# Values projected in five chunks of 128 keys and one split over column tiles, with new constants for the order of the work

## The chip, the core and the metric

The kernel runs on one core of a Trainium2 chip. A core has a matrix engine (PE, whose weight loads are listed apart as PEld), a vector engine (DVE), a scalar engine (ACT), a general engine (POOL) and a queue that only issues transfers (SP). Each works through its own list of instructions in order; semaphores hold an instruction until what it needs is there. The metric is the device time of one execution in microseconds (us); lower is better. The kernel before takes 619.33 us, the median of three runs (619.13, 619.33 and 622.4).

## The reference

One layer of cross-attention and one FFN over 8 batches of 100 queries and 722 context rows (keys), 512 features, 16 heads of 32. The attention weights come from sparsemax, not softmax: each row of scores is cut at a bound tau so that what lies above it sums to one.

```
def sparsemax(x):
    x = x - jnp.max(x, axis=-1, keepdims=True)
    zs = -jnp.sort(-x, axis=-1)
    L = x.shape[-1]
    rho = jnp.arange(1, L + 1, dtype=x.dtype)
    cssv = jnp.cumsum(zs, axis=-1) - 1.0
    support = zs > cssv / rho
    k = jnp.maximum(jnp.sum(support, axis=-1, keepdims=True), 1)
    tau = jnp.take_along_axis(cssv, k - 1, axis=-1) / k.astype(x.dtype)
    return jnp.clip(x - tau, 0.0)
...
vh = _split_heads(v @ Wv + bv)
scores = jnp.einsum('bhqd,bhkd->bhqk', qh, kh) * scale
attn = sparsemax(scores)
out = jnp.einsum('bhqk,bhkd->bhqd', attn, vh)
return out @ Wo + bo
...
real = jnp.einsum('bti,io->bto', x, jnp.cos(theta + theta_noise))
imag = jnp.einsum('bti,io->bto', x, jnp.sin(phi + phi_noise))
return jnp.sqrt(real * real + imag * imag)
...
x = x + xattn(layernorm(x), ctx_1024, ctx_1024, ...)
x = x + ffn(layernorm(x), ...)
```

## The kernel before

**Steps of a batch.** Tokens are normalised in tiles of 128 rows that run over batch borders (`TILES`), transposed and multiplied into queries. The context comes in transposed, features on the partitions. The steps of one batch, with the engine that does each:

- keys (PE, line 559): for each of four groups of features and two halves of the keys, four matmuls of 361 columns, with a bias copy on ACT (line 570). In batch 0 the first six of these run as the context arrives (line 548).
- scores, called fill (PE, lines 606 and 617): 32 by 32 tiles of the array, sixteen at a time, into one large PSUM tile `psc`. Five fills a batch. ACT copies each into `s_t` (line 628, two buffers).
- tops (DVE, line 639): 8 largest of every segment of 30 or 31 scores, 312 instructions a batch, then rests, candidates and a first bound (lines 648 to 697).
- five rounds to the bound of sparsemax: compare on DVE (`above`, line 706), product on POOL (line 711), count and sum on DVE (lines 717 and 727), small updates (lines 728 to 732).
- parts: POOL splits the bounds into three bfloat16 parts (lines 747 to 764), PE transposes them (line 769), ACT copies them out (lines 778 to 793).
- values (PE, line 581): the keys are cut into 6 chunks, five of 121 and one of 117 (`CK`, `NC`). A chunk is four accumulating matmuls, the chunk's context columns as the stationary operand, 512 feature columns moving. ACT copies the chunk to `v_t` (line 594).
- weights (PE, lines 813 and 826): minus the bound, then keys times queries on four row tiles, five pairs of feature group and key chunk a time (`PAIRS`), with the keys on the partitions. ACT takes the relu (line 838).
- outputs (PE, line 849): weights times values on four column tiles of 32 features each; ACT adds the bias (line 863).
- once a token tile is complete: output product, residual, second norm, two FFN products (line 502), squares on ACT, sum on POOL, root on ACT, result on POOL and its transfer out.

The weights of the FFN are made on POOL and ACT in the first batches (lines 419 to 437). After the loop the program tests whether the bounds were safe, and has a slower second path for the case that they weren't.

**Order.** A planner (`Plan`) writes out one order for all engines before anything is issued. A step is a `Task` with an engine and a cost from the table `STEPS`; edges say what it waits for, and `hold` says which buffers it takes and who frees them (four PSUM banks `pm`, one `psc`, and so on). A greedy loop takes, engine by engine, the step that can start first, and among those the one due first. The due time is the batch number times `PERIOD`, less the length of the longest chain behind the step, plus a constant for its kind from `LAG`; `STAY` is what a PE step gains in that comparison when it has the same tiling as the one before it (`SHAPE`). So the constants change only the order in which each engine meets its instructions, and, with the order, who waits for whom. The values of a batch are needed only by its outputs, so the planner is free to lay them between other PE work. Weights need the relu of the batch before in ACT and the one `psc`, so between weights and their outputs PE is given another product.

Of the kernel before, what the change touches and what calls it, by code (L numbers as in the profile page):

```python
# [11 lines left out]
FP = mybir.dt.float32  # L12
# [8 lines left out]
B, Q, S, DM = 8, 100, 722, 512  # L21
HD = 32
P = 128
NG = DM // P
# [19 lines left out]
def fills_of(left_first):  # L44
# [112 lines left out]
LAG = {  # L157
    "above": 260.0,
    "above count": -180.0,
    "above values": -150.0,  # L160
    "add bo": -5.0,
    "bounded": -75.0,
    "candidates": -190.0,
    "checks": 30.0,
    "deviation": 165.0,
    "ffn": 300.0,
    "fill": -240.0,
    "fill copy": 30.0,
    "fill last": -235.0,
    "first bound": 270.0,  # L170
    "keys": -65.0,
    "keys bias": 280.0,
    "keys part": -285.0,
    "leftovers": 250.0,
    "load bias": 205.0,
    "load ctx": 295.0,
    "load part": 120.0,
    "load w": 200.0,
    "load x": -160.0,
    "load x again": 180.0,  # L180
    "losses": 250.0,
    "normed": -80.0,
    "normed 2": -110.0,
    "normed T": -65.0,
    "normed copy": -245.0,
    "output product": 235.0,
    "outputs": -205.0,
    "outputs bias": 70.0,
    "parts": -180.0,
    "parts T": -165.0,  # L190
    "parts copy": -240.0,
    "parts copy last": -285.0,
    "queries": -285.0,
    "queries bias": -215.0,
    "residual": -55.0,
    "rests": 130.0,
    "result": 150.0,
    "sines": -300.0,
    "square": -215.0,
    "square sum": 275.0,  # L200
    "stats": 100.0,
    "stats 2": 265.0,
    "tops": 240.0,
    "turned": 160.0,
    "turns": -255.0,
    "update": 55.0,
    "update far": 155.0,
    "values": 110.0,
    "values copy": -200.0,
    "weights": -80.0,  # L210
    "weights relu": 300.0,
}


# [108 lines left out]
def xattn_ffn(  # L323
# [18 lines left out]
    nc = tc.nc  # L342
# [7 lines left out]
    ps1 = ctx.enter_context(tc.tile_pool(name="ps1", bufs=4, space=PSUM))  # L350
# [224 lines left out]
        )  # L575

    def values(st, c):
        n = min(CK, S - c * CK)
        st["pv", c] = pv = ps1.tile([P, DM], FP, name="pm")
        for k in range(NG):  # L580
            nc.tensor.matmul(  # L581
                pv[:n],
                lhsT=st["c"][:, k, c * CK : c * CK + n],
                rhs=wv_sb[:, k, :],
                start=(k == 0),
                stop=(k == NG - 1),
            )

    def values_copy(st, c):

        if "v" not in st:
            st["v"] = big.tile([P, NC, DM], FP, name="v_t")
        n = min(CK, S - c * CK)
        nc.scalar.copy(st["v"][:n, c, :], st.pop(("pv", c))[:n])  # L594

# [369 lines left out]
    for b in range(B):  # L965
# [239 lines left out]
    with tc.If(flag > 0):  # L1205
        with tc.For_i(0, B) as b:
# [20 lines left out]
            for c in range(NC):  # L1227
                values(st, c)
                values_copy(st, c)
            st["top"] = top = small.tile([P, NT], FP, name="top")  # L1230
            st["t", 0] = t_all = small.tile([P, NT], FP, name="t_all", bufs=1)
            st["th"] = small.tile([P, NC3 + 1, HG], FP, name="th")
# [96 lines left out]
```

## Time and profile before

| | |
|---|---|
| median of three runs | 619.33 us |
| profiled execution, its own time | 617.21 us |
| its span | 615.6 us |
| PE busy | 590.9 us (96%), 6497 matmul records |
| DVE busy | 520.5 us (85%) |
| ACT busy | 257.5 us (42%) |
| POOL busy | 226.3 us (37%) |
| granted PE clock over the span | 0.994 |
| values, matmuls (line 581) | 384 records, mean 600 ns |
| values, copies (line 594) | 48, mean 586 ns |
| outputs (line 849) | 1536 records, mean 251 ns |

The span is the stretch that the profiler covers. Busy is the time in which at least one instruction of an engine ran; matmuls overlap, so the mean of a record is longer than its share of the busy time, and the distance from one group's first record to the next group's is a better price. Each fp32 matmul leaves two records. The chain of waits, followed back from the last instruction, runs 46% through PE and 39% through DVE, in turns.

### The profile page before, as it was taken

The page shows a single profiled execution, that of the slowest core. Times are in us where ns is not written, and L with a number is a line of the kernel's source. Part 1 is how long each engine was busy: PE and PEld are TensorE (multiplying, and loading weights), DVE is VectorE, ACT ScalarE, POOL GpSimd, SP SyncE. Part 2 cuts the span into 40 slices and gives each one's busy share as a digit, 9 for nine tenths or more (in the row PEclk, how much of TensorE's full clock was granted, in tenths as well). Part 3 has the DMA queues.
Part 4 walks back from the last instruction along what each step waited for, and adds up shares of the span by engine and source line. Part 5 has one row for each costly group of instructions (what it writes and reads, how often), then busy time and mean ns, then how long its engine had stood idle before and what let it go on. Part 6 is the DMA issues. An engine that isn't in the chain of part 4 may idle for free.

```text
span 615.6 us, 17162 instructions
## 1 busy us (share of the span) xinstructions
PE 590.9 (96%) x6497; PEld 330.5 (54%) x6497; DVE 520.5 (85%) x3198; ACT 257.5 (42%) x355; POOL 226.3 (37%) x296
## 2 busy tenths in 40 slices
PE   5999999899999999999999999999999999999974
PEld 3755445556555655566466644675457434555531
DVE  2079999999999999997899989998999899998210
ACT  1244542355354435441644343552545334443521
POOL 1688487765500450024311650025211440165021
PEclk9999999999999999999999999999999999999998
DMA  8920012002000110002010102000030000000000
GB/s 307 364 92 19 18 56 78 18 19 98 19 2 3 40 60 2 3 2 97 19 37 2 41 2 98 3 2 1 3 132 3 0 23 2 2 20 2 2 18 21
DMA packets 12264, 26.56 MB, mean 43 GB/s; under 512 B 1856, under 2 KB 1856, under 8 KB 12176
## 3 DMA queue, kind: packets, MB, share of 16 engines
q1 hardware_dynamic: 11664, 23.77, 11.3%
q0 software_dynamic: 512, 1.64, 0.7%
q8 instruction: 53, 0.87, 0.6%
q14 instruction: 35, 0.29, 0.2%
HBM read 23.76 MB, written 1.64 MB: 41 GB/s over the span
## 4 chain that ended last, share of the span: by engine, by line
PE 46%; DVE 39%; issue 7%; POOL 5%; ACT 1%; DMA 1%; SPq 0%; POOLq 0%; DVEq 0%; ACTq 0%
DVE cand L639 19%; PE pm L581 12%; PE pm L559 12%; PE pm L502 5%; DVE f L727 4%; DVE m L706 4%; PE psc L826 3%; PE pm L849 3%; PE psc L617 3%; DVE n L717 3%; PE pm L479 3%; POOL p L711 3%; PE psc L548 2%; DVE rest L648 1%; DVE t L674 1%
## 5 line engine op out<-in xcount | busy, mean ns | idle before, releaser
L639 DVE MAX8 cand<-s_t 128x8 f32<-128x30 f32 x2496 | 230.3, 174 | 3.5 <-ACT s_t L628 3.5
L711 POOL TENSOR_TENSOR p<-z,m 128x1040 f32<-128x1040 f32 (+2 forms) x50 | 89.1, 1785 | 271.4 <-DVE m L706 269.7
L581 PE MATMUL pm<-wv_sb,c_t 128*121 128x512 f32 (+1 forms) x384 | 174.7, 600 | 0.0
L559 PE MATMUL pm<-c_t,wk_sb 128*128 128x361 f32 x464 | 150.9, 473 | 0.0
L559 PEld LDWEIGHTS pm<-c_t,wk_sb 128*128 128x128 f32 x464 | 84.5, 189 | 52.3 <-issue 7.6
L581 PEld LDWEIGHTS pm<-wv_sb,c_t 128*121 128x121 f32 (+1 forms) x384 | 67.2, 183 | 82.8 <-issue 78.3
L838 ACT ACTIVATE aT<-psc 121x2000 f32<-121x2000 f32 (+1 forms) x40 | 70.8, 1771 | 53.6 <-PE psc L826 53.6
L628 ACT COPY s_t<-psc 128x1924 f32<-128x1924 f32 (+2 forms) x40 | 69.0, 1725 | 47.9 <-DVE cand L639 23.7
L594 ACT COPY v_t<-pm 121x512 f32<-121x512 f32 (+1 forms) x48 | 28.1, 586 | 93.8 <-PE pm L581 93.8
L570 ACT ACTIVATE k_t<-pm,bk_sb 128x361 f32<-128x361 f32 x60 | 33.6, 565 | 71.1 <-PE pm L559 70.9
L727 DVE TENSOR_REDUCE f<-p 128x13 f32<-128x1040 f32 (+2 forms) x50 | 50.7, 1013 | 9.5 <-POOL p L711 9.5
L717 DVE TENSOR_REDUCE n<-m 128x13 f32<-128x1040 bf16 (+2 forms) x50 | 50.7, 1013 | 1.1
L826 PE MATMUL psc<-q_t,k_t 32*121 32x100 f32 (+1 forms) x1536 | 46.8, 262 | 0.0
L849 PEld LDWEIGHTS pm<-aT,v_t 121*32 121x32 f32 (+1 forms) x1536 | 32.7, 109 | 24.7 <-issue 21.7
L826 PEld LDWEIGHTS psc<-q_t,k_t 32*121 32x121 f32 (+1 forms) x1536 | 45.9, 180 | 0.2
L617 PE MATMUL psc<-k_t,q_t 32*32 32x481 f32 (+1 forms) x1536 | 43.2, 474 | 0.0
L849 PE MATMUL pm<-aT,v_t 121*32 121x100 f32 (+1 forms) x1536 | 41.7, 251 | 1.2 <-ACT aT L838 1.2
L479 PEld LDWEIGHTS pm<-hT,wq_sb 128*128 128x128 f32 x224 | 28.2, 191 | 8.2 <-issue 6.3
L479 PE MATMUL pm<-hT,wq_sb 128*128 128x128 f32 (+1 forms) x224 | 29.5, 277 | 0.0
L502 PE MATMUL pm<-cos_sb,hT 128*128 128x512 f32 (+1 forms) x56 | 27.5, 636 | 0.7 <-ACT hT L469 0.7
L518 POOL TENSOR_TENSOR sq<-sq 128x512 f32<-128x512 f32 (+1 forms) x7 | 8.8, 1264 | 48.7 <-ACT sq L515 48.6
L617 PEld LDWEIGHTS psc<-k_t,q_t 32*32 32x32 f32 x1536 | 13.9, 103 | 23.1 <-issue 15.4
(298 smaller groups left out, 570.9 us busy)
## 6 DMA issues: line engine op xcount, KB each, us to landing
c_t<-in_ctx SPq DMA_DIRECT2D x7, 1444.0 KB, 6.3
x_t<-in_x SPq DMA_DIRECT2D x12, 256.0 KB, 2.9
out<-sq POOLq DMA_DIRECT2D x6, 256.0 KB, 2.9
c_t<-in_ctx SPq DMA_DIRECT2D x4, 361.0 KB, 6.2
wk_sb<-in_L_xattn_Wk SPq DMA_DIRECT2D x4, 256.0 KB, 5.5
wq_sb<-in_L_xattn_Wq SPq DMA_DIRECT2D x4, 256.0 KB, 6.3
cos_sb<-in_L_ffn_theta SPq DMA_DIRECT2D x4, 256.0 KB, 3.9
n_t<-in_L_ffn_theta_noise SPq DMA_DIRECT2D x4, 256.0 KB, 3.6
```

The source lines that it names most:

```text
L479: nc.tensor.matmul(tk["pq"][:, g, : tk["n"]], lhsT=wq_sb[:, c, g * P : (g + 1) * P], rhs=tk["hT"][:, c, :], start=(c == 0), stop=(c == NG ...
L559: nc.tensor.matmul(pk, lhsT=wk_sb[:, c, g * P : (g + 1) * P], rhs=st["c"][:, c, i * SH : (i + 1) * SH], start=(c == 0), stop=(c == NG - 1),)
L581: nc.tensor.matmul(pv[:n], lhsT=st["c"][:, k, c * CK : c * CK + n], rhs=wv_sb[:, k, :], start=(k == 0), stop=(k == NG - 1),)
L617: nc.tensor.matmul(psc[b * HD : (b + 1) * HD, j, at : at + EDGE[hi] - EDGE[lo]], lhsT=st["q"][r, g, qb * HD : (qb + 1) * HD], rhs=st["k"][ ...
L628: nc.scalar.copy(s_t[:, :, :n], st["psc"][:, :, :n])
L639: nc.vector.max(st["cand"][:, n, k, :], st["s", f][:, j, at + EDGE[k] - first : at + EDGE[k + 1] - first],)
L711: nc.gpsimd.tensor_tensor(st["p"][:, lo:hi], st["z"][:, lo:hi], st["m"][:, lo:hi], ALU.mult)
L717: nc.vector.tensor_reduce(n_t, st["m"][:, lo:hi], AX.X, ALU.add)
L727: nc.vector.tensor_reduce(s_t, st["p"][:, lo:hi], AX.X, ALU.add)
L826: nc.tensor.matmul(psc[:m, j, k * Q : (k + 1) * Q], lhsT=st["k"][r, g, lo : lo + m], rhs=st["q"][r, g, :], start=False, stop=(k == len(PAI ...
L838: nc.scalar.activation(st["aT", n][:CK, :, :w], st["psw"][:CK, :, :w], AF.Relu, scale=SCALE)
L849: nc.tensor.matmul(st["po", g][j * HD : (j + 1) * HD, :Q], lhsT=st["v"][:m, c, f : f + HD], rhs=aT[:m, j, k * Q : (k + 1) * Q], start=(c = ...
```

## The change

The values are cut into five chunks of 128 keys and a last one of 82. The 82 are computed as 64 keys and then 18 keys. For the 64, the array is used as two column tiles of 64: both have the same 64 keys, and each computes half of the 512 features, so its result has 64 partitions and 256 columns in PSUM, the two halves one below the other. For the 18, four column tiles of 32 each compute a quarter of the features (128 columns). Copying it out now takes six ACT copies, which also move the halves and quarters back side by side. The last chunk becomes a kind of its own for the planner (`values last`), its copy waits for the first chunk's copy, and the cost of a fill over two groups is set higher. `STAY`, `PERIOD` and nearly all of `LAG` have new values. Weights, relu and outputs follow `CK` and `NC`: chunks of 128 keys and one of 82 (`S - 5 * 128`).

```
-CK = 121
+CK = P
 NC = 6
+CL = S - (NC - 1) * CK
+CA = 64
+CB = CL - CA
...
+    "values last": ("PE", 2.7),
+    "values last copy": ("ACT", 2.0),
...
-SHAPE = {"fill": 1, "fill last": 2, "outputs": 2, "weights": 3}
+SHAPE = {"fill": 1, "fill last": 2, "outputs": 2, "values last": 2, "weights": 3}
-STAY = 175.0
-PERIOD = 121.0
+STAY = 50.0
+PERIOD = 96.0
...
-    "values": 110.0,
-    "values copy": -200.0,
-    "weights": -80.0,
-    "weights relu": 300.0,
+    "values": 220.0,
+    "values copy": 20.0,
+    "values last": 195.0,
+    "values last copy": 100.0,
+    "weights": -40.0,
+    "weights relu": -95.0,
...
     def values(st, c):
-        n = min(CK, S - c * CK)
         st["pv", c] = pv = ps1.tile([P, DM], FP, name="pm")
         for k in range(NG):
             nc.tensor.matmul(
-                pv[:n],
-                lhsT=st["c"][:, k, c * CK : c * CK + n],
+                pv,
+                lhsT=st["c"][:, k, c * CK : (c + 1) * CK],
                 rhs=wv_sb[:, k, :],
...
+    def values_last(st):
+        st["pv", NC - 1] = pv = ps1.tile([P, DM], FP, name="pm")
+        lo = (NC - 1) * CK
+        for m, n, at in ((CA, CA, 0), (CB, HD, DM * CA // P)):
+            w = DM * n // P
+            for k in range(NG):
+                for j in range(P // n):
+                    nc.tensor.matmul(
+                        pv[j * n : j * n + m, at : at + w],
+                        lhsT=st["c"][:, k, lo : lo + m],
+                        rhs=wv_sb[:, k, j * w : (j + 1) * w],
+                        start=(k == 0),
+                        stop=(k == NG - 1),
+                    )
+            lo += m
...
+    def values_last_copy(st):
+        pv = st.pop(("pv", NC - 1))
+        for lo, m, n, at in ((0, CA, CA, 0), (CA, CB, HD, DM * CA // P)):
+            w = DM * n // P
+            for j in range(P // n):
+                nc.scalar.copy(
+                    st["v"][lo : lo + m, NC - 1, j * w : (j + 1) * w],
+                    pv[j * n : j * n + m, at : at + w],
+                )
...
-                    tiles=FS,
+                    tiles=FS * (1.0 if len(cs) == 1 else 1.4),
...
-            v = add("values", lambda st=st, c=c: values(st, c), *c_in, *w["v"])
-            e = add("values copy", lambda st=st, c=c: values_copy(st, c), v)
+            if c < NC - 1:
+                v = add("values", lambda st=st, c=c: values(st, c), *c_in, *w["v"])
+                e = add("values copy", lambda st=st, c=c: values_copy(st, c), v)
+            else:
+                v = add("values last", lambda st=st: values_last(st), *c_in, *w["v"])
+                e = add("values last copy", lambda st=st: values_last_copy(st), v, vs[0])
```

More of the change, by code (lines that the diff above doesn't have):

```diff
@@ L149 @@
 }
-SHAPE = {"fill": 1, "fill last": 2, "outputs": 2, "weights": 3}
+SHAPE = {"fill": 1, "fill last": 2, "outputs": 2, "values last": 2, "weights": 3}
 CHANGE = (0.19, 0.1, 0.1, 0.1)
-STAY = 175.0
-PERIOD = 121.0
+STAY = 50.0
+PERIOD = 96.0
 WINDOW = 0.0
 LAG = {
[L158 to L178, printed above, removed]
-    "load x": -160.0,
[L180 to L207, printed above, removed]
-    "values": 110.0,
-    "values copy": -200.0,
-    "weights": -80.0,
-    "weights relu": 300.0,
@@ new lines @@
+    "above count": 105.0,
+    "above values": -195.0,
+    "add bo": 55.0,
+    "bounded": 300.0,
+    "candidates": 230.0,
+    "checks": 235.0,
+    "deviation": 40.0,
+    "ffn": 200.0,
+    "fill": -115.0,
+    "fill copy": -275.0,
+    "fill last": -110.0,
+    "first bound": -85.0,
+    "keys": -70.0,
+    "keys bias": -120.0,
+    "keys part": -100.0,
+    "leftovers": -270.0,
+    "load bias": -60.0,
+    "load ctx": 215.0,
+    "load part": -100.0,
+    "load w": -105.0,
+    "load x": -160.0,
@@ new lines @@
+    "load x again": 110.0,
+    "losses": 285.0,
+    "normed": 300.0,
+    "normed 2": -190.0,
+    "normed T": -165.0,
+    "normed copy": -195.0,
+    "output product": 285.0,
+    "outputs": -115.0,
+    "outputs bias": 115.0,
+    "parts": -115.0,
+    "parts T": -125.0,
+    "parts copy": 240.0,
+    "parts copy last": -265.0,
+    "queries": -295.0,
+    "queries bias": -130.0,
+    "residual": -60.0,
+    "rests": 5.0,
+    "result": -225.0,
+    "root": -20.0,
+    "sines": 285.0,
+    "square": 185.0,
@@ L212 @@
+    "square sum": 20.0,
+    "stats": 20.0,
+    "stats 2": 125.0,
+    "tops": 230.0,
+    "turned": -10.0,
+    "turns": 250.0,
+    "update": 120.0,
+    "update far": 85.0,
+    "values": 220.0,
[4 more added lines that the diff above has]
+    "weights relu": -95.0,
 }
@@ L592, in values_copy @@
             st["v"] = big.tile([P, NC, DM], FP, name="v_t")
-        n = min(CK, S - c * CK)
-        nc.scalar.copy(st["v"][:n, c, :], st.pop(("pv", c))[:n])
+        nc.scalar.copy(st["v"][:, c, :], st.pop(("pv", c)))
+    def values_last_copy(st):
[7 more added lines that the diff above has]
+                )
     def fill(st, f):
@@ L1226, in xattn_ffn @@
                     keys_bias(st, g, i)
-            for c in range(NC):
+            for c in range(NC - 1):
                 values(st, c)
                 values_copy(st, c)
+            values_last(st)
+            values_last_copy(st)
             st["top"] = top = small.tile([P, NT], FP, name="top")
```

## The prediction

> **What bounds the kernel now.** The profiled execution spans 615.6 us; its own time is 617.21 us, so 1.6 us lie around the span. The three timed runs have a median of 619.33 us, 2.1 us above that execution. I make the sum against 617.2 and carry the difference over to the median.
>
> I read first the busy time of each engine in three stretches. They are cut where DVE starts the first search for maxima (36 us) and where it ends the last bound (569 us). After the length of a stretch the columns are PE, PEld, DVE, ACT and POOL.
>
> ```profile
> 0.00:36.00 36.00, 28.97 (x140) 18.58 (x141) 7.50 (x34) 8.79 (x16) 15.59 (x30) 1.00 0.87 310
> 36.00:569.00 533.00, 528.68 (x6000) 294.19 (x6002) 507.04 (x3147) 234.68 (x320) 203.04 (x253) 1.00 0.08 28
> 569.00:616.00 47.00, 33.25 (x370) 17.73 (x362) 5.92 (x18) 14.03 (x20) 7.69 (x14) 0.92 0.04 13
> ```
>
> In the middle PE is idle for 4.3 us and DVE for 26 of 533. Both engines are full, so an edit that relieves one alone is soon stopped by the other. The waits of DVE inside that stretch say how much of the 26 us PE causes:
>
> ```profile
> DVE f L727 <- POOL p L711: 9.5, 15, 1.3
> DVE cand L639 <- ACT s_t L628: 3.5, 4, 1.5
> DVE x_t L511 <- PE pm L502: 1.8, 1, 1.8
> DVE h_t L455 <- PE pm L463: 1.0, 1, 1.0
> ```
>
> The first row is DVE waiting for POOL inside the bound iteration; no PE work is behind it. The other three are products and score copies that came late, 6.3 us in all. In the other direction PE waits for DVE at the transposes of the bounds, in the timeline:
>
> ```profile
> 118.99 0.40 PE L769 MATMUL pm<-ident_b,t 128*128 128x128 bf16 x4 [2.00 <-POOL t L762]
> 367.26 0.40 PE L769 MATMUL pm<-ident_b,t 128*128 128x128 bf16 x4 [1.30 <-POOL t L762]
> ```
>
> After 569 us the end is PE's: rounds of weights and outputs of the last batch, with other products laid between them, then the last norm and the last two FFN products. Its timeline, with the third round of the last batch in the first two rows:
>
> ```profile
> 574.53 1.20 PE L826 MATMUL psc<-q_t,k_t 32*121 32x100 f32 x40
> 577.75 1.07 PE L849 MATMUL pm<-aT,v_t 121*32 121x100 f32 x40 [0.92 <-ACT aT L838]
> ...
> 589.57 0.90 PE L849 MATMUL pm<-aT,v_t 121*32 121x100 f32 x32
> ```
>
> **The price of the new last chunk.** A value chunk now costs what the chain of waits shows, 8 records (each matmul is recorded twice):
>
> ```profile
> 34.52 3.43 PE pm L581 x8
> ...
> 190.68 3.62 PE pm L581 x8
> ```
>
> The first is followed by work in the same tiling, the second by the outputs on four column tiles: 0.19 us more. A 512-column record is 3.43/8 = 0.43 us.
>
> Five chunks keep their four matmuls of 512 columns; 128 keys instead of 121 change only the number of output rows. The last chunk becomes 16 records of 256 columns on two column tiles and 32 of 128 columns on four. By columns a record is 0.214 and 0.107 us. If the tiles run side by side, this is 16 x 0.214 / 2 + 32 x 0.107 / 4 = 1.71 + 0.86 = 2.57 us. That four tiles do so the outputs rows show: 40 records end 1.07 us after the first starts, 32 after 0.90, so one more costs 21 ns, a quarter of the 84 ns that 100 columns take at the rate above. The fixed part is 1.00 (the distance to the next group) - 40 x 0.021 = 0.17 us; I charge it once for the change between the two tilings: 2.74 us. No row has two tiles of 64. The bounds are 2.57 (no charge) and 4.45 us (those two strictly in turn, 1.71 more); I take 2.74, nearest to the four-tile rows. Saved: 3.43 - 2.74 = 0.69 us, x8 = 5.5 us of PE.
>
> I counted the tiling changes in both built orders. A 128-wide product before outputs falls from 40 to 35 times, since in some rounds the new chunk stands there instead (5 x 0.19), and before weights or scores from 49 to 45 (4 x 0.095, half as much): 1.3 us. PE's own sum falls by 6.8 us.
>
> Weights now load 128, 128, ..., 82 keys instead of 121, ..., 117. The sum of key columns per head is 722 either way, so I cost these 192 records a batch at nothing; a record there takes 26 ns (40 end after 1.20, 32 after 0.99 us). Were each of the 160 with 128 keys to cost 7/121 more with nothing gained on the 82, it would be 0.24 us a batch, 2 us lost; were the 32 shorter in proportion and the others not longer, 2 us gained.
>
> **The copies.** One copy of 512 columns (586 ns, 48 in all) becomes, in the last chunk, two of 256 and four of 128. Copies of 16 columns take 162 ns and of 512 columns 586, so by the line through them 0.37 and 0.26 us: 1.8 us instead of 0.59, 9.7 us of ACT over eight batches. ACT is busy for 235 of 533 us in the middle. Where the chunk stands between weights and outputs, the copies start 2.74 us after the weights end and last till 4.6; a copy of outputs takes 0.34; the next weights end at 2.74 + 1.00 + 1.35 = 5.1. They just fit. If the fixed part were that of the 100-column rows (0.34 for 128 columns) they would end 0.5 us later and hold the next relu by some 0.2 us, in at most eight places: 0 to 1.6 us.
>
> Here the Trainium skill speaks against the change: its page "TensorEngine Tiling (Array Packing)", section "PSUM Bottleneck", says that tiling speeds up the matmuls but not the emptying of PSUM, which may become the bottleneck. Were each added 1.2 us on the path, 9.7 us would be lost, and by the sum below the change would end near 625. The row above, ACT idle for more than half of the middle stretch, is why I don't use it. The page "TensorE: Matmul & The Clock Gate", section "Measured speedup vs the span model", gives 2.38 for three column tiles, 0.79 of ideal; an estimate by that is 2.57 / 0.79 = 3.25 us, which would leave little of the saving. The 21 ns of the outputs rows contradict it here.
>
> **The order, place by place.** I ran prices like these along PE in both orders and compared.
>
> *Start.* Loads: x, two wk, then the first context part, which keeps fourth place on SP's queue; the tiles of x behind the first fall to places 20 and later. Their norm work has slack in the old profile except in one respect: DVE's statistics of tiles 3 and 4 (0.86 us each) and one normalisation (0.72) ran while DVE had nothing else, and now stand between its first maxima: +2.4 us in DVE's full stretch. Against that PE reaches the first scores 2.1 us earlier, because one keys product (2.43) moved behind them and one transpose (0.4) ahead. The bias on the queries takes back 0.2. DVE starts 1.9 earlier and has 2.4 more to do: +0.5 us at the end of batch 0. PE, 0.8 earlier there by its sum, then waits 3.3 instead of 2.0 us at the transposes: 1.3 lost.
>
> *Batches 1 to 4.* PE's sum is 3.5 us shorter at the first scores of batch 4, net of that loss 2.2. DVE's waits of 1.05, 1.82 and 1.54 us lie before or at this point, so DVE takes this gain: -2.2. In batch 4 small steps (residual, statistics) now stand inside the bound iterations and cover two of the three waits for POOL there (0.8 each): DVE -3.8.
>
> *Batches 4 to 6.* PE reaches the transposes of batch 4 5.3 us earlier by its sum but must wait for DVE: -3.8, so 1.5 lost in all. At the scores of batch 6 PE's sum is 5.0 shorter, net 3.5; DVE waited 1.01 there and follows: -3.5.
>
> *Last batch.* PE's sum to the third round of weights is 6.4 us shorter; less 1.5 lost, less about 1.4 because the second round now has only transposes between weights and outputs: -3.5. The round needs DVE's third group: 568.8 - 3.5, plus the step from there on POOL and ACT (about 3.2), is 568.5, or 570.6 if the residual of batch 5, now behind two instead of seven batches of maxima, waits about 2.1 us for its product. PE is there at 574.3 - 3.5 = 570.8, so PE decides, narrowly. From there on the old kernel needed 16.1 us to the last output product (574.3 to 590.4). The new one has two rounds with a product between (2 x 5.97) and one bare (1.13 + 1.7 wait + 0.83) : 15.6. Another 0.4. The remaining 25 us are the same chain.
>
> **Sum.** -3.5 - 0.4 = -3.9 us: 613.3 for an execution like the profiled one, 615.4 for the median. Its own range is 613 to 618: 2 us either way for the uncertain crossings.
>
> **The rivals.** *DVE takes nothing back.* The waits of 1.05 to 1.82 us are replaced by others of the same size, DVE keeps its +0.5, and batch 5's residual adds 2.1. Its third group then ends near 571.4, and with 3.2 the third round starts at 574.6, as before: 619 to 620. For it: DVE is full and its instructions are the same in number. Against: three PE waits are where PE gets earlier. *More gain.* The crossings at batches 0 and 4 cost nothing, and the chunk costs 2.57: 6.8 + 1.3 (8 x 0.17) - 1.7 for the bare round = -6.4: 613. Against: PE already waits for DVE at both crossings. *Slower: the two 64-wide tiles run in turn.* Then the chunk is 4.45 us, 1.02 more than before; x8 less 1.3 is +6.9 us of PE, nothing of the gain above is left, and the time is 626. It decides from the point where the 64-key part takes more than 2.4 us instead of 1.71. For it: no row shows this tiling. Against: the 21 ns. *Slower: the copies hold the relu or the score copies* by their full 1.2 us in every batch: -3.9 + 9.7 less what was slack, 622 to 625.
>
> **How the numbers follow.** Forecast 0.50, no gain 0.22, more gain 0.08, tiles in turn 0.08, copies 0.12. What a measurement of this kernel can tell from no change is about 0.5%, 3.1 us: faster means below 616.2, slower above 622.4. Of the forecast some 0.39 lies below 616.2 and 0.11 above; with more gain that is 0.47 faster. Same is 0.11 + 0.20 = 0.31. Slower is 0.22. The range 612 to 623 leaves out the tiles in turn, part of the copies, and little below.
>
> **What would show it.** The new matmuls should take about 2.7 us from first to next group; over 3.4 and the tiles don't overlap. The wait of PE at the first transposes should grow from 2.0 to about 3.3 us. DVE's three waits for PE should shrink. DVE's last bound should end near 565.3 instead of 568.8, and the third round of weights start near 570.8. Wrong makes it above all a new wait of DVE for the residuals or for score copies behind the six copies, which I priced from rows of another order.

## The result and the profile after

The changed kernel takes 627.25 us (median of four, 625.22 to 629.71) against 619.29 us before: a ratio of 1.0124, 95% interval 1.0099 to 1.015. It is 8 us slower. I had forecast 615.4 us, and the time lies above my range of 612 to 623 as well.

The profiled execution took 625.22 us, with a span of 623.5 (before: 617.21 and 615.6). So I compare these two, 8.0 us apart. Of these, 1.5 us lie behind the last matmul: from its record to the end of the span it is 8.6 us before and 10.1 after. The other profiles of this case have 8.6 to 10.4 us there in either order, so this part is not the order's. First the busy time of each engine in the changed kernel, cut at the same two events as before: DVE's first search for maxima and its last bound (now near 572 us). The columns are the same as before: length, PE, PEld, DVE, ACT, POOL, then PE's granted clock, DMA share and GB/s.

```profile
0.00:36.00 36.00, 29.49 (x177) 19.62 (x178) 7.76 (x44) 8.94 (x15) 15.88 (x30) 1.00 0.89 311
36.00:572.00 536.00, 528.37 (x6234) 300.61 (x6217) 508.52 (x3136) 243.66 (x358) 200.35 (x253) 0.99 0.09 28
572.00:622.00 50.00, 33.27 (x424) 18.97 (x422) 6.30 (x20) 13.94 (x22) 7.75 (x15) 0.90 0.04 13
```

The middle is 3 us longer, and PE is idle in 7.6 us of it instead of 4.3. Its clock column is no longer 1.00. Although the matmuls were made cheaper, PE's busy time did not fall: 591.1 us in all, 590.9 before. The groups by shape say that the price of the chunk is not the reason (columns: matmuls, shape, number of records, then busy us and mean ns of a record):

```profile
L587 PE MATMUL pm<-wv_sb,c_t 128*128 128x512 f32 x320 | 146.7, 605 | 0.0
L603 PE MATMUL pm<-wv_sb,c_t 128*64 128x256 f32 x128 | 15.6, 385 | 0.0
L603 PE MATMUL pm<-wv_sb,c_t 128*18 128x128 f32 x256 | 8.6, 274 | 0.0
```

By these rows a plain chunk has 146.7 / 40 = 3.67 us of busy time, and a new last chunk (15.6 + 8.6) / 8 = 3.03. So 0.64 us is saved eight times. The first place where time was lost is the first transposes of the bounds. PE in the timeline (start, duration, what it does, and in brackets the wait before it):

```profile
114.56 2.59 PE L566 MATMUL pm<-c_t,wk_sb 128*128 128x361 f32 x8
122.17 0.61 PE L801 MATMUL pm<-ident_b,t 128*128 128x128 bf16 x4 [5.02 <-POOL t L794]
122.57 5.13 PE L566 MATMUL pm<-c_t,wk_sb 128*128 128x361 f32 x8
127.63 0.39 PE L845 MATMUL psc<-tT,neg_b 3*128 3x500 bf16 x4
```

Two things stand here. PE waits 5.02 us, where it waited 2.00 before. Then the same eight records of keys take 5.13 us that had taken 2.59 just ahead of the wait. Cut into stretches, the clock column shows why:

```profile
117.20:122.20 5.00, 0.03 (x1) 0.04 (x2) 4.97 (x43) 0.55 (x1) 2.13 (x9) 0.85 0.12 41
122.20:125.00 2.80, 2.80 (x8) 1.82 (x9) 2.80 (x32) 1.02 (x5) 2.72 (x5) 0.50 0.37 91
125.00:127.60 2.60, 2.60 (x5) 1.01 (x3) 2.60 (x31) 0.00 (x0) 1.98 (x4) 0.51 0.02 6
127.60:131.00 3.40, 3.40 (x52) 2.58 (x52) 3.37 (x32) 2.38 (x2) 3.11 (x4) 1.00 0.02 5
```

After the wait PE is granted half its clock, and gets it back only at 127.6 us. The first weights of batch 0 start 5.8 us later than before (127.63 against 121.80). DVE, in the same place, shows where the long wait comes from:

```profile
111.48 1.94 DVE L738 TENSOR_TENSOR m<-z,t0 0_1372 128x1040 bf16<-128x1040 f32 x1
113.34 0.14 DVE L460 RECIPROCAL rs<-sd 32x1 f32<-32x1 f32 x1
113.59 2.34 DVE L462 TENSOR_SCALAR h_t<-x_t,mv,rs 32x512 f32<-32x512 f32 x1
115.85 1.22 DVE L749 TENSOR_REDUCE n<-m 128x13 f32<-128x1040 bf16 x1
```

and POOL:

```profile
113.49 2.16 POOL L743 TENSOR_TENSOR p<-z,m 128x1040 f32<-128x1040 f32 x1 [1.18 <-DVE rs L460]
```

The normalisation of tile 3, a small step (32 rows), now stands between the compare and the count of a bound round. There it starts beside POOL's product and ends only after it: 2.34 us. In the kernel before it stood between two rounds (at 91.84), with POOL idle, and took 0.54. So the count and all that follows it are late by 1.8 us. The kernel before has such a pair as well, in a later batch, DVE and then POOL:

```profile
342.42 2.40 DVE L455 TENSOR_SCALAR h_t<-x_t,mv,rs 128x512 f32<-128x512 f32 x1
342.38 2.16 POOL L711 TENSOR_TENSOR p<-z,m 128x1040 f32<-128x1040 f32 x1 [1.45 <-DVE rs L453]
```

There the normalisation has four times as many rows and takes as long; 128 rows take 0.55 us elsewhere.

The last batch is the second place. PE there, from the second round of weights on:

```profile
573.46 1.23 PE L858 MATMUL psc<-q_t,k_t 32*82 32x100 f32 x40
574.62 0.23 PE L801 MATMUL pm<-ident_b,t 128*128 128x128 bf16 x1
578.08 1.05 PE L470 MATMUL pm<-ident,h_t 128*128 128x128 f32 x4 [3.23 <-DVE h_t L462]
579.06 1.90 PE L881 MATMUL pm<-aT,v_t 82*32 82x100 f32 x40
580.89 0.60 PE L845 MATMUL psc<-tT,neg_b 3*128 3x200 bf16 x8
581.28 1.33 PE L858 MATMUL psc<-q_t,k_t 32*128 32x100 f32 x40
```

and ACT, which works its list in order:

```profile
576.86 0.29 ACT L456 ACTIVATE sd<-mv,estepst 128x1 f32<-128x1 f32 x1 [4.19 <-DVE mv L452]
577.06 1.82 ACT L870 ACTIVATE aT<-psc 128x2000 f32<-128x2000 f32 x1
```

The weights end near 574.7, but their relu starts at 577.06, since the deviation of the last second norm stands ahead of it in ACT's list and waits for DVE's statistics. PE waits 3.23 us, and the outputs behind that take 1.90 us instead of 1.07: half clock again. In the clock's record of the changed kernel four such stretches lie ahead of the very end: 6.8 us from 120.7, and 3.4 us each from 369.9, 578.1 and 605.4. Before, there was one, 3.4 us from 598.3.

### The profile page after: what moved, and what is told of

It reads as the page before. It is cut to its first block, busy times and chain, and to the rows that moved or that the text cites. A ratio compares the mean times of both kernels' runs of the same rounds, so it can differ in the third digit from the quotient of the medians.

```text
span 623.5 us, 17844 instructions
## 1 busy us (share of the span) xinstructions
PE 591.1 (95%) x6817; PEld 339.2 (54%) x6817; DVE 522.6 (84%) x3198; ACT 266.5 (43%) x395; POOL 224.0 (36%) x296
## 4 chain that ended last, share of the span: by engine, by line
PE 55%; DVE 34%; issue 4%; POOL 3%; ACT 1%; DMA 1%; SPq 0%; POOLq 0%; DVEq 0%; ACTq 0%
DVE cand L671 17%; PE pm L566 15%; PE pm L587 11%; PE pm L509 5%; PE psc L858 5%; PE pm L881 4%; PE psc L649 4%; DVE m L738 3%; PE pm L486 3%; DVE f L759 3%; DVE n L749 2%; PE psc L555 2%; PE pm L603 2%; PE psc L845 1%; POOL p L743 1%
## 5 line engine op out<-in xcount | busy, mean ns | idle before, releaser
L566 PE MATMUL pm<-c_t,wk_sb 128*128 128x361 f32 x464 | 153.5, 479 | 0.0
L587 PE MATMUL pm<-wv_sb,c_t 128*128 128x512 f32 x320 | 146.7, 605 | 0.0
L587 PEld LDWEIGHTS pm<-wv_sb,c_t 128*128 128x128 f32 x320 | 58.9, 192 | 68.4 <-issue 66.6
L870 ACT ACTIVATE aT<-psc 128x2000 f32<-128x2000 f32 (+1 forms) x40 | 70.8, 1770 | 42.0 <-PE psc L858 41.4
L616 ACT COPY v_t<-pm 128x512 f32<-128x512 f32 x40 | 23.3, 586 | 71.8 <-PE pm L587 71.8
L858 PE MATMUL psc<-q_t,k_t 32*128 32x100 f32 (+1 forms) x1536 | 47.5, 264 | 0.0
L858 PEld LDWEIGHTS psc<-q_t,k_t 32*128 32x128 f32 (+1 forms) x1536 | 46.7, 181 | 0.5
L881 PEld LDWEIGHTS pm<-aT,v_t 128*32 128x32 f32 (+1 forms) x1536 | 33.7, 111 | 21.8 <-issue 19.0
L881 PE MATMUL pm<-aT,v_t 128*32 128x100 f32 (+1 forms) x1536 | 42.4, 254 | 1.7 <-ACT aT L870 1.7
L509 PE MATMUL pm<-sin_sb,hT 128*128 128x512 f32 (+1 forms) x56 | 25.7, 602 | 0.0
```

Of the source, the lines that this page charges most:

```text
L509: nc.tensor.matmul(tk[name], lhsT=tk[lhs][:, c, :], rhs=w_sb[:, c, :], start=(c == 0), stop=(c == NG - 1),)
L566: nc.tensor.matmul(pk, lhsT=wk_sb[:, c, g * P : (g + 1) * P], rhs=st["c"][:, c, i * SH : (i + 1) * SH], start=(c == 0), stop=(c == NG - 1),)
L587: nc.tensor.matmul(pv, lhsT=st["c"][:, k, c * CK : (c + 1) * CK], rhs=wv_sb[:, k, :], start=(k == 0), stop=(k == NG - 1),)
L858: nc.tensor.matmul(psc[:m, j, k * Q : (k + 1) * Q], lhsT=st["k"][r, g, lo : lo + m], rhs=st["q"][r, g, :], start=False, stop=(k == len(PAI ...
L870: nc.scalar.activation(st["aT", n][:CK, :, :w], st["psw"][:CK, :, :w], AF.Relu, scale=SCALE)
L881: nc.tensor.matmul(st["po", g][j * HD : (j + 1) * HD, :Q], lhsT=st["v"][:m, c, f : f + HD], rhs=aT[:m, j, k * Q : (k + 1) * Q], start=(c = ...
```

## The experiments

Three theories were on the table. A: the chunk does what it should, and the new order costs the time, in part (A1) by the normalisation inside the bound round. B: the chunk, its copies or the 128-key weights cost it. C: what follows the long waits, the half clock, takes a large share. All ratios are to the kernel before, run beside on the same chip.

| run | median us | ratio, 95% interval |
|---|---|---|
| changed kernel | 627.25 | 1.0124 (1.0099 to 1.015) |
| new chunk, order of before | 616.88 | 0.9945 (0.9916 to 0.9974) |
| old chunk, new order | 628.4 | 1.0155 (1.0132 to 1.0177) |
| normalisation moved out | 623.13 | 1.0069 (1.0052 to 1.0087) |
| products in the first long wait | 625.67 | 1.0111 (1.0088 to 1.0133) |
| transposes of the last batch moved | 627.67 | 1.0127 (1.009 to 1.0165) |
| both these moves | 626.61 | 1.0116 (1.0078 to 1.0154) |
| the tail's moves with the deviation | 624.74 | 1.0076 (1.0047 to 1.0106) |
| normalisation and tail's moves | 622.25 | 1.0053 (1.0033 to 1.0073) |
| these, products at the end | 621.3 | 1.0037 (1.0012 to 1.0062) |
| these, products in three waits | 616.27 | 0.9944 (0.9929 to 0.9959) |
| these, products in five waits | 616.53 | 0.9946 (0.9933 to 0.9959) |
| new order unmoved, products (three misplaced) | 625.16 | 1.0082 (1.0062 to 1.0101) |
| new order unmoved, products in four waits | 620.72 | 1.0016 (0.9993 to 1.004) |
| before, products at the end | 617.0 | 0.9975 (0.9957 to 0.9994) |
| new chunk, order of before, copies moved | 615.25 | 0.9932 (0.9915 to 0.9948) |
| the same, products at the end | 612.89 | 0.9902 (0.9876 to 0.9928) |

**The two halves of the change apart.** The constants, costs and tilings of before with the new chunk (the edit is shown against the changed kernel; the values of `LAG` go back too):

```
-STAY = 50.0
-PERIOD = 96.0
+STAY = 175.0
+PERIOD = 121.0
...
-                    tiles=FS * (1.0 if len(cs) == 1 else 1.4),
+                    tiles=FS,
...
```

> The order of the kernel before, step for step on every engine, with the new last chunk, its six copies and the 128-key weights in place of the old. Theory A (the chunk is worth its price, the loss lies in the new order): the chunk takes 2.76 to 2.88 us in the trace of the changed kernel where the old one took 3.43 to 3.63, so PE has 8 x 0.65 = 5 us less to do; PE and DVE are both full, so 2 to 5 us of it reach the end: 614 to 617. Theory B (the chunk itself costs, through its copies or the weights of 128 keys): 624 or more.

It took 616.88 us (612.03 to 620.08): 2.7 us faster than before. Then the new order with six old chunks:

```
-CK = P
+CK = 121
...
     def values_last(st):
+        values(st, NC - 1)
...
```

> The order of the changed kernel, step for step, with six chunks of 121 keys and one copy each as before. Theory A: all of the loss and the saving of the chunk on top: 627 + 2 to 5 = 629 to 632. Theory B: back to the kernel before, 618 to 621.

It took 628.4: 9 us slower than before, with no new chunk in it. So B falls: the order costs the time. The chunk gives something in the order of before; in the new order the 1.1 us between 628.4 and 627.25 are not clear of noise, since the two intervals overlap. The first kernel shows the one place where the copies hold anything up. ACT:

```profile
144.00 2.56 ACT L444 ACTIVATE sin_sb<-sin_sb,zero_b 128x512 f32<-128x512 f32 x4
146.47 1.80 ACT L625 COPY v_t<-pm 64x256 f32<-64x256 f32 x6
148.30 0.34 ACT L897 ACTIVATE oT<-pm,bv_sb 128x100 f32<-128x100 f32 x1
148.54 1.50 ACT L872 ACTIVATE aT<-psc 128x1600 f32<-128x1600 f32 x1
```

The six copies take the 1.80 us of my estimate. They stand behind the sines of the FFN weights, and the relu behind both is late: PE waits 2.56 us at 150.1, and the clock halves for 3.4 us.

**The start.** The new order, with tile 3's normalisation behind the bounds of batch 0 instead of inside their round:

```
+        move("normed", 3, 0, "update", 0, -1)
```

> The changed kernel with one DVE step moved: the normalisation of token tile 3, which stands between a comparison and the count of batch 0's last bound iteration and there takes 2.34 us instead of 0.54, comes after that iteration. Theory A1 (this step makes batch 0's bounds late, PE waits 5.02 us for them and its clock is halved for 6.8 us after that wait): the wait falls to about 2.7 us, the first weights start at 122 to 124 instead of 127.6 us, and the kernel gains 3 to 5 us: 622 to 624. Theory A2 (batch 0 is made up later, since PE and DVE hold each other up further on anyway): under 1 us gained, 626 to 627.

It took 623.13, 4.1 us less than the changed kernel. Its profile, PE and then DVE:

```profile
119.99 0.61 PE L801 MATMUL pm<-ident_b,t 128*128 128x128 bf16 x4 [2.79 <-POOL t L794]
120.39 4.09 PE L566 MATMUL pm<-c_t,wk_sb 128*128 128x361 f32 x8
```

```profile
111.58 1.94 DVE L738 TENSOR_TENSOR m<-z,t0 0_1372 128x1040 bf16<-128x1040 f32 x1
113.55 1.24 DVE L749 TENSOR_REDUCE n<-m 128x13 f32<-128x1040 bf16 x1
118.02 0.55 DVE L462 TENSOR_SCALAR h_t<-x_t,mv,rs 32x512 f32<-32x512 f32 x1
```

In its new place the same instruction takes 0.55 us instead of 2.34, and the wait of PE falls by 2.23 us, to 2.79. The keys behind it still take 4.09 instead of 2.6 us. To see what the clock alone does there, the wait was kept and filled with five extra products of 512 columns whose result nobody reads:

```
+        warm_at = [t for t in order if t.kind == "parts T" and t.batch == 0][0]
...
+            pw = ps1.tile([P, DM], FP, name="pm")
+            for k in range(5):
+                nc.tensor.matmul(
+                    pw, lhsT=wk_sb[:, k % NG, :P], rhs=wv_sb[:, k % NG, :],
...
```

> The changed kernel with five extra products of 512 columns (4.3 us, results unused) on PE ahead of the transposes of batch 0's bounds, inside the wait of 5.02 us. Theory C (the half clock after the wait costs by itself): the clock stays whole, the keys product after the transposes takes 2.6 us instead of 5.1, the first weights start 2.5 us earlier at 125, and the kernel ends 1 to 2.5 us earlier: 624.5 to 626. If only the wait matters: 627.

It took 625.67, with the first weights at 125.0 instead of 127.6 and no half clock until the last batch. Of the 2.6 us won there 1.6 show in the median, as theory C said; but the interval overlaps with that of the changed kernel, so this run alone does not settle it.

**The last batch.** The transposes that PE waited for were put behind the third weights, alone and with the move of the normalisation:

```
+        move("normed T", 6, -1, "weights", 7, 2)
+        move("normed copy", 6, -1, "normed T", 6, -1)
```

> The changed kernel with one PE step moved: the transposes of the second norm of tile 6, which stand ahead of the second outputs of the last batch and wait 3.2 us for DVE's normalisation there, come behind the third weights, as in the old order. Theory A: the wait and the half clock after it (3.4 us and more) go; 2 to 5 us gained: 622 to 625. Rival (the third weights wait for DVE's last bounds anyway): 626 to 627.

> The changed kernel with both moves: tile 3's normalisation behind the bounds of batch 0, and tile 6's transposes behind the third weights. Theory A: the two gains add, 4.1 + 2 to 5: 618 to 621. If the second place only takes over what the first gave: 622 to 623.

Both missed: 627.67 and 626.61. The wait did not go, it went one step on, to the outputs, whose relu still stood behind the waiting deviation. The second of these kernels in steps of 4 us:

```profile
570.00:574.00 4.00, 1.72 (x57) 1.38 (x49) 2.43 (x9) 0.26 (x2) 1.08 (x6) 1.00 0.01 4
574.00:578.00 4.00, 2.19 (x48) 1.89 (x52) 0.71 (x2) 1.97 (x4) 0.00 (x0) 0.56 0.01 2
578.00:582.00 4.00, 3.33 (x49) 2.75 (x45) 0.00 (x0) 0.69 (x2) 0.00 (x0) 0.50 0.00 0
582.00:586.00 4.00, 4.00 (x5) 1.80 (x6) 0.00 (x0) 1.87 (x2) 0.00 (x0) 0.50 0.00 0
586.00:590.00 4.00, 4.00 (x60) 1.86 (x58) 0.00 (x0) 0.86 (x2) 0.00 (x0) 0.73 0.01 4
```

PE is half idle for 8 us, and from 574.5 on it is at half clock for 13.7: in this execution, the longest of four (624.8 to 629.0), what the first move had gained is lost again here. So the deviation, with the normalisation that needs it, was moved behind the relu as well. This was run together with tile 3's normalisation ("three moves" from here on: that, the deviation, the transposes) and without it:

```
+        move("deviation", 6, -1, "weights relu", 7, 1)
+        move("normed 2", 6, -1, "deviation", 6, -1)
+        move("normed T", 6, -1, "weights", 7, 2)
+        move("normed copy", 6, -1, "normed T", 6, -1)
```

> The changed kernel with its order repaired in two places: the normalisation of tile 3 behind batch 0's bounds, and in the last batch ACT's deviation of the last second norm (with the normalisation and the transposes that need it) behind the relu of the second round. Theory: the tail lost its gain because that relu stood behind a deviation that waited for statistics, PE waited 4.1 us and its clock then halved for 10 to 14 us. Without it the wait ahead of the second outputs is that of a bare round, about 2 us, the clock halves for at most 3.4 us there, and the time is 617 to 620, the normalisation's move alone having given 623.1. Rival (the loss of the tail is not the clock's but the late statistics', which something needs anyway): the wait moves behind to the transposes and the time stays at 622 to 624.

> The changed kernel with the tail's moves alone (deviation, normalisation and transposes of the last second norm behind the relu and the weights). Theory: the tail's half clock goes, some 3 to 5 us: 622 to 624.5. Rival (the tail does not matter beside the start): 626 to 628 as with the transposes moved alone, 627.7.

They took 622.25 and 624.74. The wait became what a bare round has, as the theory said:

```profile
570.00 0.23 PE L801 MATMUL pm<-ident_b,t 128*128 128x128 bf16 x1
572.09 1.75 PE L881 MATMUL pm<-aT,v_t 82*32 82x100 f32 x40 [1.87 <-ACT aT L870]
```

The times are above what I expected. The 622.25 lies where the rival had put it, but the rival's mechanism is not there: no wait moved to the transposes, which now follow the third weights at once. What stays behind the wait of 1.87 us is 3.4 us at half clock. Against the move of tile 3's normalisation alone (ratio 1.0069, 1.0052 to 1.0087) the 1.0053 (1.0033 to 1.0073) is not a clear gain, since the intervals overlap. Against the changed kernel both moves together gain 5 us.

**The end of all kernels.** Before and after alike, the last two FFN products run behind a wait for the last norm. Three extra products in that wait, in the kernel before:

```
+        if tk is tks[-1] and "py" in tk:
+            for k in range(3):
+                nc.tensor.matmul(
+                    tk["pt"].rearrange("p c r -> p (c r)"), lhsT=wk_sb[:, k, :P], rhs=wv_sb[:, k, :],
...
```

> The kernel before with the three extra products ahead of the last norm's transposes alone. Theory of the half clock: the first of the last two products takes 3.5 instead of 5.4 us, 1.5 to 2 us gained: 617.5 to 618. If only waits matter: 619 to 620.

617.0, 2.3 us less than the 619.28 beside it. The same with the new chunk in the order of before, where the six copies of batch 1 were also put behind the last relu of batch 0 (`move("values last copy", 1, 0, "weights relu", 0, -1)`), and that move alone:

> The new chunk in the old order, with two further edits. The six copies of batch 1's last chunk, which stand behind the second sine step and ahead of the last relu of batch 0, go behind that relu; and three extra products of 512 columns (2.6 us, overwritten by the transposes after them) run in the wait of 2.93 us before the last norm's transposes. Theory: the wait of 2.56 us before batch 0's last outputs goes back to 0.3 and its half clock with it (2 to 3 us), and the first of the last two FFN products takes 3.5 instead of 5.4 to 6.7 us: 611 to 614 against 616.9. If half clock does not matter: 616 to 617.

> The order of before with the new chunk, and batch 1's six copies moved behind the last relu of batch 0; no extra products at the end. It splits the 4.0 us between 616.9 (chunk alone) and 612.9 (chunk, this move, products at the end). Theory: the products gave 2.3 us in the kernel before, so the move gives the rest: 614.5 to 615.7. Rival (what the move gives is spent elsewhere): 616.5 to 617.

612.89 and 615.25. The first is faster than both kernels of the case, by 1.0% against before (ratio 0.9902, 0.9876 to 0.9928). Its end shows the products (line 471) and, behind them, the last eight at full clock; the kernel with the chunk alone needed 6.66 us for the row that takes 3.70 here:

```profile
590.73 2.74 PE L471 MATMUL pm<-wv_sb,wk_sb 128*128 128x512 f32 x6
593.73 0.66 PE L476 MATMUL pm<-ident,h_t 128*128 128x128 f32 x4 [0.26 <-DVE h_t L462]
595.06 3.70 PE L515 MATMUL pm<-cos_sb,hT 128*128 128x512 f32 x8 [0.68 <-ACT hT L482]
```

**Clock and waits apart.** The new order with its three moves, first with products at the end, then also in the waits of batches 0 and 4, then in five places:

> The three moves in the changed kernel's order, and three extra products of 512 columns ahead of the last norm's transposes so that the last eight run at full clock. Theory: some 2.3 us less than with the moves alone, 614.5 to 618. Rival (no dip is left to remove at the end): equal to the moves alone.

> The three moves, and extra products of 512 columns that keep PE at work in its three long waits: three ahead of the first transposes of the bounds in batch 0, two in batch 4 and three before the last norm's transposes; the waits stay. With the moves and the last three products alone it was 621.3. Theory (each wait costs itself and then a stretch at half clock): two stretches of 3.4 us go, 1.7 us each, so 617 to 618.5, and what then stays against the order of before with the new chunk (616.9 without such products, 612.9 with them) is the waits themselves. Rival (the half clock has little to do with the 4 to 5 us that the moves left): 620.5 to 622.

> As the run before with three moves and products in three waits (616.3, but 615.0 to 621.5 between executions, the profiled one among the longest, with 10 us at half clock in the last batch), and two products more ahead of the outputs of the last batch's second and last rounds, where PE still waits 1.9 and 1.7 us. Theory (the spread between executions comes from those waits): 614 to 615.5, and all executions within 2 us. Rival (the spread has another cause): 616 and a spread as wide.

621.3, 616.27 and 616.53. The first is a miss: the end alone gave 1 us, not 2.3, and the intervals of the two kernels overlap. The second is better than its theory. The last has the same median, so its theory fell for the time, and the rival had that right; its six executions lie closer (615.4 to 617.5 instead of 615.0 to 621.5 in seven), which is what the theory said of the spread.

Last, the new order with nothing moved, and products in its waits:

> The changed kernel in its own order, nothing moved, with extra products of 512 columns that keep PE at work in its long waits: five ahead of the first transposes of the bounds in batch 0, two in batch 4, three ahead of the last batch's second-norm transposes and three ahead of the last norm's. Theory (of the 8 us that the change lost, and the gain that the chunk should have brought, the half clock takes about half): four stretches go, 17 us at half clock, of which the first gave only 1.6 alone: 618 to 621. Rival (the waits and the order of the work take it, the clock little): 623 to 625.5.

> The run before with products in an unmoved order (625.2) put three of its products ahead of the first norm's transposes of tile 6, where PE did not wait (2.74 us of PE at 360.4), and not ahead of the last batch's second-norm transposes. Here they stand there, in the wait of 3.26 us. Theory (what the clock alone takes of the change's loss is some 5 to 6 us of 8): 2.7 us of PE and half of a 3.4 us stretch go, 620.5 to 622. Rival (DVE is the bound there and takes the 2.7 us up; the clock alone is worth little, waits and order take the rest): 623.5 to 625.5.

In the first, three products stood where PE was not waiting, ahead of the first norm's transposes of tile 6, and cost PE 2.74 us:

```profile
360.38 2.74 PE L1242 MATMUL pm<-wv_sb,wk_sb 128*128 128x512 f32 x6
```

It took 625.16 and settles nothing. With them in place it took 620.72, as the theory said. Its first wait, filled (line 1242), and the keys behind it at full clock:

```profile
116.01 4.45 PE L1242 MATMUL pm<-wv_sb,wk_sb 128*128 128x512 f32 x10
121.24 0.40 PE L807 MATMUL pm<-ident_b,t 128*128 128x128 bf16 x4 [0.78 <-POOL t L800]
121.47 2.65 PE L572 MATMUL pm<-c_t,wk_sb 128*128 128x361 f32 x8
```

Its order is that of the changed kernel, step by step, and it has more work. Yet it is 6.5 us faster.

## Why the prediction was wrong

Put side by side, the medians make an account (they come from several sets of runs, in which the kernel before had 619.2 to 620.0):

| | as it is | clock kept up by products |
|---|---|---|
| before | 619.3 | 617.0 |
| new chunk, order of before, copies moved | 615.3 | 612.9 |
| changed kernel | 627.3 | 620.7 |
| changed, three moves | 622.3 | 616.3 |

The first two rows have products in the wait at the end alone, the third in four waits, the last in three. Read downwards on the right, the chunk (with its moved copies) gives 4.1 us, the new order takes 7.8 back, and the moves return 4.4 of these. Read across, filling the waits gives the kernel before 2.3 us and the changed one 6.5. So of the 8 us of the result about 4 are waits and order, net of the chunk's gain, and about 4 the clock that those waits cost. By the intervals above each of these differences is uncertain by 1 to 2 us, and in the kernel before the clock is not kept up throughout: its profile with products at the end still has 3.4 us at half clock in batch 0.

*The chunk.* Right. I took 2.74 us from group to group; the changed kernel has 2.76 ahead of outputs and 2.88 ahead of weights. The two 64-wide tiles run side by side, so that rival is out. In the order of before it brings 2.7 us (616.88 against 619.55 beside it), and 4.8 with the copies out of the way of one relu (615.25 against 620.03); the intervals of the two ratios overlap.

*The weights with 128 keys.* No cost was seen. A full group of 40 is 1.14 to 1.19 us to the next, mostly 1.13 to 1.15 before, but the step ahead of it (minus the bound) is as much shorter: the two together take 1.39 us in the mean, 1.40 before.

*The copies.* Right in size: 1.80 us. That they hold the relu in every batch (my fourth rival) did not happen; in the order of before they did so once.

*Start.* This is the step that failed: "DVE starts 1.9 earlier and has 2.4 more to do: +0.5 us at the end of batch 0." Up to the bounds it held. DVE started its maxima at 34.0 instead of 35.9, and its bounds of batch 0 at 73.98 against 73.92 before. But the last bound came at 119.92 instead of 116.73, 3.2 us later, because the bound rounds themselves took 3.1 us more. The sum has no term for them. The normalisation that it charges with 0.72 us is another one, tile 2's, which moved from the start to between the maxima and cost there what I had put. That of tile 3 moved inside the rounds, from a place where POOL was idle to one beside POOL's product, and I put this at nothing: it took 2.34 instead of 0.54, 1.8 of the 3.1 us. The rest lies in small steps of DVE and was not taken apart. With that one step out of the way the wait of PE is 2.79 us, below the 3.3 that I had put there, and the kernel takes 4.1 us less. So the 5.02 comes from this. The row of 2.40 us at 342.42 in the old profile could have told me.

*The clock, which no step of the prediction has.* I counted a wait of PE at its length. The runs show that its price has a second part, the half clock behind it. The row of the last stretch in my own prediction had a clock of 0.92, and products in the wait of the old end gave 2.3 us: the evidence was in the table that I had read for its busy times.

*Batches 1 to 4.* DVE was to lose three waits for PE. The residual's shrank from 1.82 to 0.93 us and that for the score copies of batch 4 from 1.54 to 1.06; the normalisations' are 1.0 in sum as before. DVE came to the maxima of batch 4 at 297.7 instead of 296.2, still 1.6 us late, and behind that point new waits came up (columns: waited in all, times, longest; 9.0 of the first row and 2.1 of the second lie in the start):

```profile
DVE q_t L499 <- PE pm L486: 12.8, 2, 9.0
DVE cand L671 <- ACT s_t L660: 7.0, 4, 2.9
DVE f L759 <- POOL p L743: 6.9, 11, 0.8
DVE h_t L462 <- PE pm L470: 1.0, 2, 0.7
```

The new ones are 3.77 us for queries of batch 6 and 2.87 for the score copies of the last batch. The waits for POOL, of which I had seen two covered, fell from 9.5 to 6.9.

*Batches 4 to 6.* I had PE wait little at the transposes of batch 4 (1.5 us lost in all at both crossings). It waits 1.91 there and then runs its values at half clock: eight records take 5.25 us, the next eight 3.70.

*Last batch.* DVE's last bound came at 572.3, not 565.3, and the third round of weights at 580.9, not 570.8. I had charged 1.4 us for the second round, which "now has only transposes between weights and outputs". The wait is 3.23 and is ended by DVE's normalisation, not by a relu alone: with the output product gone from that place, ACT's deviation ahead of the relu is on the path. In the kernel before the deviation stands one round later in ACT's list, ahead of the third relu. There it waited 0.93 us, and the relu behind it had to wait for its weights anyway. The kernels with the transposes moved and those with the deviation moved too separate this: the wait stays at 4.1 us as long as the deviation is ahead, and falls to 1.87 once it isn't.

*The rivals.* "DVE takes nothing back" had the right direction (DVE keeps its delay of the start), but ended at 619 to 620. None had a wait that costs more than its length. Two slips in my working (40 x 0.021 from 1.00 leaves 0.16, not 0.17; 15.6 from 16.1 leaves 0.5, not 0.4) change nothing.

What stays open: with the clock kept up and three moves, the new order is still 3.4 us behind the order of before (616.3 against 612.9). DVE's new waits for queries and score copies are in the trace; that they are the cause was not tried. That POOL's product is what holds the normalisation is read from the rows of all traces (last section) and from the move that took the two apart; no run changed POOL's product alone.

## What to carry to other kernels

Here the order was worth more than the cheaper step. Price a small step that is moved by the duration it has beside its new neighbours, and look whose list it heads. Price a wait of the matrix engine at its length plus the half clock that may follow, and read the clock column of every stretch first. When a wait can't be removed, a few products that nobody reads, put exactly into it, are cheap; a few places off they cost their full time.

## What the runs showed of the hardware

*The clock.* The clock's record of the 18 profiles here has two values, 1.00 and 0.50, and each stretch at 0.50 but the last of a run lasts 3.413 us or two, three or four times as long. Waits of 5.02, 3.23, 2.84 and 1.91 us in the changed kernel came with half clock behind them, as did one of 2.56 with the chunk alone; those of 2.00 and 1.30 before, and one of 1.69 ahead of the last outputs after, did not. The same wait can go either way. In the run with misplaced products, and in that with both moves, the one of 1.69 had it: the outputs behind it took 1.56 us instead of 0.90. The kernel before with products at its end has the order of before up to there; its wait of 1.99 at batch 0's transposes had it too, and the eight records of keys behind took 4.01 us instead of 2.65. The half clock need not start at once: behind the wait of 1.91 it came 1.6 us after PE had gone on. The starts of the four stretches (120.7, 369.9, 578.1, 605.4) are 73, 61 and 8 times 3.413 us apart, so they lie on a fixed raster. Whether a wait costs something by where it falls on that raster stays open: no run shifted a wait to test it, and the waits of 2.00 and 1.99 both begin within 0.1 us of a mark of the raster, with different outcome.

The time of one program goes with the clock as well: with three moves and products in three waits, the mean granted clock was 0.995 in the five executions of 615.0 to 616.6 us, 0.992 in that of 618.4 and 0.987 in that of 621.5.

The Trainium skill, in "TensorE: Matmul & The Clock Gate", Part 1, has the half rate, the free-running window of about 3.4 us and the return to full rate after a busy one, and the traces agree with all three. It names an idle window of about 3.4 us as the condition; here 1.9 us were enough, and in two runs 1.7, and the measurement decides.

*DVE beside POOL.* The normalisation of tile 3 took 2.34 us beside POOL's product and 0.55 us alone. This is no single pair. In the 18 traces 48 normalisations start while this product runs; they take 0.72 to 2.41 us, and every one ends 0.28 or 0.29 us after the product. The other 204 take 0.53 to 0.59 us, but for 13 beside another operation of POOL (0.87 to 0.91). The Trainium skill, in "SBUF — State Buffer", section "Who interferes with whom", says that these two engines share a pair of ports, that an operation of this kind can need it, and that the later one then waits for the whole instruction of the other. The rows agree that the later one is held to the end of the product. That it then needs 0.28 us, half of what it takes alone, they do not explain.
